# Bilinear row sampling as a sum of clamped ramps over row differences, in place of a sum of hats over rows

## The chip, the cores and the metric

The kernel runs on one core of a Trainium2 chip as one launch. The metric is the device time of that launch in microseconds. A core has five engines that work side by side, each through its own instructions in order: TensorE (PE in the profile, its weight loads PEld), VectorE (DVE), ScalarE (ACT), GpSimd (POOL) and SyncE (SP), which here only issues transfers.

## The reference

The reference is a network of four residual layers on x of shape (16, 32, 128, 128). Each layer adds a block of the group-normalised x. The change lies in layer 1, a deformable convolution with nine taps along a curved line. Cut to what matters:

```
x = x + L0(gn(x));  x = x + L1(gn(x));  x = x + L2(gn(x));  x = x + L3(gn(x))

def L1(input):                        # (16, 32, 128, 128)
    offset = tanh(group_norm(conv3x3(input)))
    y_off  = offset[:, :9]
    y      = weight * mamba(y_off) + rows + cumulated(y_off)   # 9 row maps
    x_new  = columns + (-4 .. 4)
    ys = clip(y, 0, 127);  xs = clip(x_new, 0, 127)
    deformed = grid_sample_bilinear(input, xs, ys)
    out = conv2d(deformed, dsc_w, dsc_b, stride=(9, 1))        # sum over 9 taps
    return group_norm(out, gn_w, gn_b, 8)
```

The columns xs are whole numbers, so the bilinear sample mixes two rows of one column. For tap k at column c it is the sum over all rows r of hat(ys - r) * input[r, c + k - 4], where hat(d) is 1 - |d| between -1 and 1 and 0 elsewhere.

## The kernel before, in words

The program runs its stages one after the other: `layer0` writes x1 to a scratch tensor in DRAM, `layer1_offsets` makes the offsets, `layer1_scan` runs the recurrence and writes the nine clipped row maps (ymap), `layer1_sample` (L1122) samples, convolves, normalises and writes x2, and layers 2 and 3 follow. x1 is kept in four tensors of 128 rows (four images of 32 channels each); one row holds a whole 128 x 128 image plane.

`layer1_sample` takes the 16 images one after the other, and each image in 32 blocks of four columns (HW // 4 = 32, numbered n; i is n modulo 4). The 128 partitions hold the image's rows r, so that a matmul contracts over rows: its weights are one column of the image (128 rows by 32 channels, from the tile xt), and its moving operand is the matrix of hats for 128 output points. Four such matmuls with different column groups fill one PSUM bank of 128 x 512.

The hats come in three ways, by tap:

- Taps 4 to 7: `fetch` (L1198) loads the row map of the block with the same 2048 numbers in all 128 partitions (tile yd, four buffers, 1 MB each). `absolutes` (L1331) lets ScalarE form |y - r| with a bias of minus the row number (nrow), and `hats` (L1215) lets VectorE form min(., 1) - 1, which is minus the hat. The convolution's weights w4 and w8 carry the factor -1.
- Taps 0 to 3: `near` (L1335) calls `spread` (L1206), where TensorE copies one row of the small tile Y to all partitions, two taps into each of two PSUM tiles pb (two buffers). ScalarE empties each with Abs into ya, and VectorE applies `hats`.
- Tap 8: `eighth` (L1340) does the same once in four blocks out of Y8, into h8.

`taps` (L1229) runs the 16 matmuls of four taps into a bank pd, and VectorE copies the bank into ds (L1371 after taps 0 to 3, L1377 after taps 4 to 7). `last_tap` (L1241) does tap 8 for four blocks, and ScalarE copies that bank (L1398). The banks pd have two buffers that go round. Once in four blocks `convolve` (L1252) multiplies with the convolution's weights, ScalarE adds the bias (oc, L1267), and one block later `turn` (L1270) transposes back to rows. `finish` (L1282) is a generator of which one step is taken per block; it normalises the previous image, adds xt (L1324) and stores x2 through POOL's queue. It runs from block 1 of the next image to block 22. xt has two buffers, and an image's buffer is given back only when `finish` has read it.

`open_image` (L1178), called at block 12 for the image after, issues the loads of Y, Y8 and xt on SP's queue. `in_order` (L1349) holds TensorE, VectorE and ScalarE to the order of the code; the order of SP's issues is left to the scheduler. The loop's body puts the work of block m in this order: taps 0 to 3 of m; Abs of yd and hats of ya for m + 1; the copy L1371; the spread of m + 2; taps 4 to 7 of m; hats of yd for m + 1; the copy L1377; then by i the convolution (0), the turn (1), the eighth tap's spread (2) or the last tap (3).

Of the kernel before, what the change touches and what calls it, by code (L numbers as in the profile page):

```python
# [68 lines left out]
def layer0(tc, w, x, x1, nb=B):  # L69
# [5 lines left out]
    with ExitStack() as ctx:  # L75
# [200 lines left out]
        def tail_z(st):  # L276
            b, t0 = st["b"], st["t0"]
            pz = ps_1.tile([P, 4, HW], F32, name="pz", tag="pz")
            for k in range(4):
                nc.tensor.matmul(pz[:, k], st["aT"][:, k], wadd, start=True, stop=False)  # L280
                nc.tensor.matmul(pz[:, k], st["mT"][:, k], wmod, start=False, stop=True)
            o = wp.tile([P, 4, HW], F32, name="o", tag="o")
            nc.vector.tensor_add(o, pz, xs[b][:, t0 : t0 + 4])
            r0 = (b % 4) * T + t0
            nc.sync.dma_start(x1[b // 4][r0 : r0 + 4].rearrange("t (c d) -> c t d", d=HW), o)

# [835 lines left out]
def layer1_sample(tc, w, x1, x2, ymap, sb1, batches=range(B)):  # L1122
# [8 lines left out]
    nc = tc.nc  # L1131
    V, S, M = nc.vector, nc.scalar, nc.tensor.matmul
    W4 = 4 * HW
    NB = HW // 4
    batches = list(batches)
    with ExitStack() as ctx:
# [8 lines left out]
        ident = load(nc, cp, w["ident"], "ident")  # L1145
        nrow = load(nc, cp, w["nrow"], "nrow")
        avg = cp.tile([P, P], F32, name="avg", tag="avg")
        V.memset(avg, 1.0 / P)

        sel = cp.tile([P, 32, P], F32, name="sel", tag="sel")  # L1150

        cb = cp.tile([P, NG, 4, 2], F32, name="cb", tag="cb")
        with tc.tile_pool(name="ct", bufs=1) as tp:
            e32 = load(nc, tp, w["eye32"], "eye32")
# [23 lines left out]
        def open_image(b):  # L1178
            im = images[b] = {}
            g, j = divmod(b, 4)  # L1180
            im["Y"] = Y = yp.tile([P, W4], F32, name="Y", tag="Y")
            nc.sync.dma_start(Y, ym(b)[0:4].rearrange("k (n f) -> (k n) f", f=W4))
            im["Y8"] = Y8 = yp.tile([P, W4], F32, name="Y8", tag="Y8")
            y8 = ym(b)[8].rearrange("(s q f) -> q s f", q=4, f=W4)
            for q in range(4):
                nc.sync.dma_start(Y8[32 * q : 32 * q + 8], y8[q])
            im["xt"] = xt = xp.tile([P, T, HW], F32, name="xt", tag="xt")
            xg = x1[g][T * j : T * j + T].rearrange("o (r c) -> r o c", c=HW)
            for q in range(4):
# [4 lines left out]
            V.tensor_scalar(w4, dw4[:, :, 0:T], s, -1.0, ALU.mult, ALU.mult)  # L1194
            im["w8"] = w8 = sp.tile([P, P], F32, name="w8", tag="w8")
            V.tensor_scalar(w8, dw8, s, -1.0, ALU.mult, ALU.mult)

# [7 lines left out]

        def spread(dst, Y, n, k):  # L1206

            for h in range(2):
                pb = psb.tile([P, 2, W4], F32, name="pb", tag="pb")
                for a in range(2):  # L1210
                    q = 32 * (2 * h + a)
                    M(pb[:, a], sel[q : q + k, n], Y[q : q + k], start=True, stop=True)  # L1212
                S.activation(dst[:, 2 * h : 2 * h + 2], pb, AF.Abs, bias=nrow)  # L1213

        def hats(t):  # L1215

            V.tensor_scalar(t, t, 1.0, 1.0, ALU.min, ALU.subtract)  # L1217

# [63 lines left out]
        def finish(b):  # L1282

            g, j = divmod(b, 4)
            im = images[b]
            ob, xt = im["ob"], im["xt"]
            st = sp.tile([P, 8, 6], F32, name="st", tag="st")
# [42 lines left out]

        def absolutes(m):  # L1331
            yd = blocks[m]["yd"]
            S.activation(yd, yd, AF.Abs, bias=nrow)  # L1333

        def near(m):  # L1335
            b, n = order[m]
            blocks[m]["ya"] = ya = hp.tile([P, 4, W4], F32, name="ya", tag="ya")
            spread(ya, images[b]["Y"], n, 32)

        def eighth(b, s):  # L1340
            h8 = hp.tile([P, 4, W4], F32, name="h8", tag="h8", bufs=2)
            spread(h8, images[b]["Y8"], s, 8)
            images[b]["h8", s] = h8

        open_image(batches[0])
        NM = len(order)
        for m in range(min(3, NM)):
            fetch(m)
        with in_order(tc, nc.tensor, nc.vector, nc.scalar):  # L1349
            eighth(batches[0], 0)  # L1350
            near(0)
            absolutes(0)
            near(1)
            hats(images[batches[0]]["h8", 0])
            hats(blocks[0]["ya"])
            hats(blocks[0]["yd"])
            done = iter(())
            for m in range(NM + 6):
                b, n = order[m] if m < NM else (None, m - NM)
                if m < NM:  # L1360
                    bl = blocks[m]
                    bl["ds"] = dp.tile([P, 2, W4], F32, name="ds", tag="ds", bufs=6)
                    if n == 12 and m + NB < NM:
                        open_image(order[m + NB][0])
                    if m + 3 < NM:
                        fetch(m + 3)
                    pd = taps(m, 0, bl["ya"])
                    if m + 1 < NM:
                        absolutes(m + 1)
                        hats(blocks[m + 1]["ya"])  # L1370
                    V.tensor_copy(bl["ds"][:, 0], pd.rearrange("p i r -> p (i r)"))  # L1371
# [5 lines left out]
                    V.tensor_copy(bl["ds"][:, 1], pd.rearrange("p i r -> p (i r)"))  # L1377
                s, i = divmod(n, 4)
# [16 lines left out]
                elif i == 3 and m < NM:  # L1395
# [3 lines left out]
                    images[b]["ds8"] = ds8  # L1399
                    if m + 1 < NM:  # L1400
                        nb_, nn = order[m + 1]
                        hats(images[nb_]["h8", nn // 4])
                next(done, None)
# [954 lines left out]
def network(ctx, tc, w, x, out):  # L2358
# [5 lines left out]

    x1 = [scratch([P, L], f"x1_{g}") for g in range(NG)]
    x2 = [scratch([P, L], f"x2_{g}") for g in range(NG)]
# [36 lines left out]
def pack(inp):  # L2403
# [203 lines left out]
```

## Time and profile before

| what | us |
|---|---|
| median of 3 runs | 16701.83 |
| lowest and highest of them | 16687.33, 16788.68 |
| the profiled execution's own time | 16668.54 |
| span in the profile | 16666.3 |
| first to last matmul of the spread (L1212) | 10735.9 to 13888.4 |
| last store issue of the sampling stage (L1325) | 13929.8 |
| SP's 14 waits for L1324 ahead of the xt loads | 64.4 |
| ScalarE's 14 waits for yd's load | 56.7 |

The span is the time from the first to the last instruction of the profiled execution. A row of the groups has the line, the engine, the operation, what it writes and reads with the shapes and the count, then the busy time in all and the mean of one in ns, then the idle time of the engine just before and what ended it. Matmuls are pipelined, so their mean is longer than their share of the time. A row of the waits has who waited, for whom, the total, how often, and the longest.

### The profile page before, as it was taken

The page shows a single profiled execution, that of the slowest core. Times are in us where ns is not written, and L with a number is a line of the kernel's source. Part 1 is how long each engine was busy: PE and PEld are TensorE (multiplying, and loading weights), DVE is VectorE, ACT ScalarE, POOL GpSimd, SP SyncE. Part 2 cuts the span into 40 slices and gives each one's busy share as a digit, 9 for nine tenths or more (in the row PEclk, how much of TensorE's full clock was granted, in tenths as well). Part 3 has the DMA queues.
Part 4 walks back from the last instruction along what each step waited for, and adds up shares of the span by engine and source line. Part 5 has one row for each costly group of instructions (what it writes and reads, how often), then busy time and mean ns, then how long its engine had stood idle before and what let it go on. Part 6 is the DMA issues. An engine that isn't in the chain of part 4 may idle for free. (4 is left out here: it accounts for less than half of the span.)

```text
span 16666.3 us, 327843 instructions
## 1 busy us (share of the span) xinstructions
PE 14464.2 (87%) x126810; PEld 5828.1 (35%) x126810; DVE 14412.7 (86%) x13784; ACT 12525.8 (75%) x25236; POOL 9711.4 (58%) x17789
## 2 busy tenths in 40 slices
PE   8998999989999888888888888899999997689966
PEld 3333333333333432222222222255555554434421
DVE  9999999999999659999999999888888886698622
ACT  8999999999999557777777777598888984466411
POOL 8999999999999457778887888500000001000012
PEclk9999999999999989999999999899899998789977
DMA  0000000000000334444454445578777876444356
GB/s 23 12 13 12 12 18 12 13 13 12 18 12 8 95 110 159 160 161 164 166 166 165 163 165 167 153 186 195 194 201 196 198 194 182 98 83 83 75 150 201
DMA packets 1347602, 1837.19 MB, mean 110 GB/s; under 512 B 161685, under 2 KB 661902, under 8 KB 1335799
## 3 DMA queue, kind: packets, MB, share of 16 engines
q1 hardware_dynamic: 1289910, 1655.23, 36.2%
q0 software_dynamic: 43840, 144.20, 2.4%
q8 instruction: 997, 16.33, 0.4%
q10 hardware_dynamic: 12288, 16.79, 0.4%
q14 instruction: 567, 4.64, 0.1%
HBM read 1497.44 MB, written 229.64 MB: 104 GB/s over the span
## 5 line engine op out<-in xcount | busy, mean ns | idle before, releaser
L235 POOL TENSOR_SCALAR Rp<-su,nv 128x128 f32<-128x128 f32 x15360 | 5406.6, 371 | 167.9 <-PE pS L241 133.0
L239 ACT ACTIVATE Ra<-su,bv 128x128 f32<-128x128 f32 x15360 | 4626.2, 390 | 406.7 <-PE pS L241 403.3
L224 DVE TENSOR_TENSOR Rd<-pu,nv 128x2048 f32<-128x2048 f32 x2176 | 4856.6, 2275 | 17.8 <-PE pS L241 16.8
L241 PE MATMUL pS<-Rd,zw 128*32 128x512 f32 x17408 | 2798.0, 606 | 378.7 <-DVE Rd L224 377.9
L919 DVE TENSOR_TENSOR_SCAN hh<-dd,state,pd 128x512 f32<-128x512 f32 x2304 | 2823.1, 1267 | 152.4 <-ACT ln L834 7.1
L940 POOL TENSOR_TENSOR hh<-hh,bc 128x2048 f32<-128x2048 f32 x512 | 2319.2, 4530 | 450.8 <-DVE state L927 439.8
L1325 POOL DMA_DIRECT2D x<-ob x64 | 92.0, 1438 | 3100.4 <-DVE ob L1324 2766.5
L904 PE MATMUL pd<-du,spread 32*128 32x512 f32 x4608 | 1340.1, 655 | 574.6 <-DVE hh L919 566.7
L896 ACT ACTIVATE dd<-dd,m_a 128x512 f32<-128x512 f32 x2304 | 1514.8, 713 | 335.3 <-DMA dd<-dm 328.9
L914 DVE TENSOR_TENSOR pd<-pd,bc 128x1024 f32<-128x1024 f32 x1152 | 1400.6, 1216 | 58.7 <-ACT bc L877 55.4
L241 PE MATMUL pS<-Rp,zw 128*32 128x512 f32 x7680 | 1314.3, 598 | 26.0 <-POOL Rp L235 25.9
L1333 ACT ACTIVATE yd<-yd,nrow 128x2048 f32<-128x2048 f32 x512 | 1238.1, 2418 | 56.7 <-DMA yd<-ymap 56.7
L1213 ACT ACTIVATE ya<-pb,nrow 128x1024 f32<-128x1024 f32 x1024 | 1196.7, 1260 | 80.6 <-PE pb L1212 80.1
L241 PE MATMUL pS<-Ra,zw 128*32 128x512 f32 x7680 | 1237.3, 601 | 0.0
L1212 PE MATMUL pb<-Y,sel 32*128 32x512 f32 (+1 forms) x5120 | 1075.3, 739 | 176.0 <-ACT ya L1213 172.8
L241 PEld LDWEIGHTS pS<-Rd,zw 128*32 128x32 f32 x17408 | 582.1, 109 | 1484.7 <-DVE Rd L224 927.4
L904 PEld LDWEIGHTS pd<-du,spread 32*128 32x128 f32 x4608 | 371.1, 189 | 1607.4 <-DVE hh L919 726.8
L1217 DVE TENSOR_SCALAR yd<-yd 128x2048 f32<-128x2048 f32 x512 | 727.5, 1421 | 207.0 <-ACT yd L1333 205.8
L1217 DVE TENSOR_SCALAR ya<-ya 128x2048 f32<-128x2048 f32 x512 | 759.0, 1482 | 10.7 <-ACT ya L1213 9.4
L1224 PE MATMUL pd<-ya,xt 128*32 128x128 f32 x16384 | 691.4, 311 | 42.5 <-DVE ds L1377 31.7
L1945 PE MATMUL ps<-t,W 128*128 128x512 f32 x1280 | 635.4, 644 | 80.9 <-DVE W L1925 53.1
L1224 PEld LDWEIGHTS pd<-yd,xt 128*32 128x32 f32 x16384 | 533.2, 178 | 471.0 <-issue 224.7
(434 smaller groups left out, 22927.2 us busy)
## 6 DMA issues: line engine op xcount, KB each, us to landing
dd<-dm SPq DMA_DIRECT2D x2304, 256.0 KB
yd<-ymap SPq DMA_DIRECT2D x512, 1024.0 KB
xq<-x SPq DMA_DIRECT2D x48, 1088.0 KB
dm<-dt POOLq DMA_DIRECT2D x192, 256.0 KB, 3.8
w<-d SPq DMA_DIRECT2D x512, 73.1 KB
xb<-tok SPq DMA_DIRECT2D x248, 144.0 KB
x<-in_x SPq DMA_DIRECT2D x64, 512.0 KB
x<-o SPq DMA_DIRECT2D x128, 256.0 KB
```

What stands on the lines that cost most here:

```text
L224: nc.vector.tensor_tensor(R, st["pu"].unsqueeze(1).to_broadcast([P, 4, 4, HW]), nv[:, :, i::32].rearrange("p t q -> p q t").unsqueeze(3).t ...
L235: nc.gpsimd.tensor_scalar(R[:, q, k], su[:, k], 3.4028234e38, nv[:, k, c], ALU.min, ALU.max)
L239: nc.scalar.activation(R[:, q, k], su[:, k], AF.Relu, bias=bv[:, k, c])
L241: nc.tensor.matmul(st["pS"][32 * q : 32 * q + 32], zw[:, 31 - i : 63 - i], R[:, q], start=first, stop=False, tile_position=(0, 32 * q), sk ...
L896: S.activation(dd[:, r], dd[:, r], AF.Exp, scale=acol[:, dr, d : d + 1])
L904: nc.tensor.matmul(pd[:, a], spread[e, k], st["du"][n][e], start=True, stop=True)
L914: V.tensor_mul(pd, pd, bm.unsqueeze(1).to_broadcast([P, 2, CH]))
L919: V.tensor_tensor_scan(hh[:, r, s], dd[:, r, s], pd[:, a, s], st["state"][:, 4 * i + r : 4 * i + r + 1], ALU.mult, ALU.add,)
L940: G.tensor_mul(hh, hh, st["bc"][1, n].unsqueeze(1).to_broadcast([P, 4, CH]))
L1217: V.tensor_scalar(t, t, 1.0, 1.0, ALU.min, ALU.subtract)
L1224: M(pd[32 * q : 32 * q + 32, i], xt[:, :, xc], h, start=True, stop=True, tile_position=(0, 32 * q),)
L1333: S.activation(yd, yd, AF.Abs, bias=nrow)
```

## The change

A sum over rows of hat(y - r) * x[r] is rewritten. With y between 0 and 127 it equals x[0] plus the sum over r of clamp(y - r, 0, 1) * (x[r + 1] - x[r]). Partitions 0 to 126 hold the differences, and partition 127 holds x[0] with a ramp that is always 1 (its entry in the bias is +1 in place of -127). To load rows 1 to 128 in one shifted transfer, `layer0` stores each plane's first row once more behind the last, so a row of x1 is 128 elements longer.

- xt is loaded shifted by a row. `differ` loads the unshifted rows a quarter at a time (tile xq) and subtracts them on GpSimd, at blocks 24 to 27 of the image before. `finish` no longer reads xt: it loads quarters of its own.
- The row number is subtracted by the spread product: one row of ones beside 16 rows of Y, and the row numbers beside the selector. Y is split into Y0 and Y1, and each group of 16 rows is loaded with its row of ones. VectorE clamps taps 0 to 3 straight out of PSUM (max 0, min 1), one instruction per pb.
- h8 is formed on ScalarE in two passes, relu(1 - v) and again relu(1 - .). Taps 4 to 7 take a Relu with the bias on ScalarE and a min with 1 on VectorE.
- The two copies of pd into ds go from VectorE to ScalarE. In the code the Relu of yd for m + 1 now stands behind the first copy and the spread of m + 2.
- GpSimd is held to the order of the code too.

```diff
@@ layer0
-            nc.sync.dma_start(x1[b // 4][r0 : r0 + 4].rearrange("t (c d) -> c t d", d=HW), o)
+            nc.sync.dma_start(x1[b // 4][r0 : r0 + 4].rearrange("t (c d) -> c t d", d=HW)[0:P], o)
+            nc.sync.dma_start(x1[b // 4][r0 : r0 + 4, L:].unsqueeze(0), o[0:1])
@@ layer1_sample, set-up
-        sel = cp.tile([P, 32, P], F32, name="sel", tag="sel")
+        sel = cp.tile([P, 16, P], F32, name="sel", tag="sel")
...
-            V.tensor_copy(sel, e32.unsqueeze(2).to_broadcast([P, 32, P]))
+            V.tensor_add(
+                sel, pick.unsqueeze(2).to_broadcast([P, 16, P]),
+                srow.unsqueeze(1).to_broadcast([P, 16, P]),
+            )
@@ open_image
-            im["Y"] = Y = yp.tile([P, W4], F32, name="Y", tag="Y")
-            nc.sync.dma_start(Y, ym(b)[0:4].rearrange("k (n f) -> (k n) f", f=W4))
-            im["Y8"] = Y8 = yp.tile([P, W4], F32, name="Y8", tag="Y8")
+            yk = ym(b)[0:4].rearrange("k (h n f) -> k h n f", h=2, f=W4)
             y8 = ym(b)[8].rearrange("(s q f) -> q s f", q=4, f=W4)
-            for q in range(4):
-                nc.sync.dma_start(Y8[32 * q : 32 * q + 8], y8[q])
+            for h, key in enumerate(("Y0", "Y1", "Y8")):
+                im[key] = Y = yp.tile([P, W4], F32, name=key, tag=key)
+                for q in range(4):
+                    p = 32 * q
+                    if h < 2:
+                        nc.sync.dma_start(Y[p : p + 16], yk[q, h])
+                    else:
+                        nc.sync.dma_start(Y[p : p + 8], y8[q])
+                        nc.sync.dma_start(Y[p + 8 : p + 16], y8[q])
+                nc.sync.dma_start(Y[16:P:32], w["one_rows"])
...
-                nc.sync.dma_start(xt[:, 8 * q : 8 * q + 8], xg[:, 8 * q : 8 * q + 8])
+                o = slice(8 * q, 8 * q + 8)
+                nc.sync.dma_start(xt[:, o], xg[1 : P + 1, o])
...
+        def quarter(b, q):
+            g, j = divmod(b, 4)
+            xq = xp.tile([P, 8, HW], F32, name="xq", tag="xq")
+            xg = x1[g][T * j + 8 * q : T * j + 8 * q + 8].rearrange("o (r c) -> r o c", c=HW)
+            nc.sync.dma_start(xq, xg[0:P])
+            return xq
+
+        def differ(b, q):
+            xt = images[b]["xt"][0 : P - 1, 8 * q : 8 * q + 8]
+            G.tensor_sub(xt, xt, quarter(b, q)[0 : P - 1])
@@ spread
-                    M(pb[:, a], sel[q : q + k, n], Y[q : q + k], start=True, stop=True)
-                S.activation(dst[:, 2 * h : 2 * h + 2], pb, AF.Abs, bias=nrow)
-        def hats(t):
-            V.tensor_scalar(t, t, 1.0, 1.0, ALU.min, ALU.subtract)
+                    M(pb[:, a], sel[q : q + 17, n], Y[q : q + 17], start=True, stop=True)
+                v = dst[:, 2 * h : 2 * h + 2]
+                if whole:
+                    V.tensor_scalar(v, pb, 0.0, 1.0, ALU.max, ALU.min)
+                else:
+                    S.activation(v, pb, AF.Relu, bias=one, scale=-1.0)
+                    S.activation(v, v, AF.Relu, bias=one, scale=-1.0)
+        def clamps(t):
+            V.tensor_scalar_min(t, t, 1.0)
@@ finish
+                xq = quarter(b, q)
...
-                V.tensor_add(ob[:, o], ob[:, o], xt[:, o])
+                V.tensor_add(ob[:, o], ob[:, o], xq)
@@ the loop
         open_image(batches[0])
+        for q in range(4):
+            differ(batches[0], q)
...
-        with in_order(tc, nc.tensor, nc.vector, nc.scalar):
+        with in_order(tc, nc.tensor, nc.vector, nc.scalar, nc.gpsimd):
...
+                    if 24 <= n < 28 and m + NB < NM:
+                        differ(order[m + NB][0], n - 24)
                     if m + 3 < NM:
                         fetch(m + 3)
                     pd = taps(m, 0, bl["ya"])
-                    if m + 1 < NM:
-                        absolutes(m + 1)
-                        hats(blocks[m + 1]["ya"])
-                    V.tensor_copy(bl["ds"][:, 0], pd.rearrange("p i r -> p (i r)"))
+                    S.copy(bl["ds"][:, 0], pd.rearrange("p i r -> p (i r)"))
                     if m + 2 < NM:
                         near(m + 2)
+                    if m + 1 < NM:
+                        ramps(m + 1)
                     pd = taps(m, 4, bl["yd"])
                     if m + 1 < NM:
-                        hats(blocks[m + 1]["yd"])
-                    V.tensor_copy(bl["ds"][:, 1], pd.rearrange("p i r -> p (i r)"))
+                        clamps(blocks[m + 1]["yd"])
+                    S.copy(bl["ds"][:, 1], pd.rearrange("p i r -> p (i r)"))
...
-                        hats(images[nb_]["h8", nn // 4])
@@ network, pack
-    x1 = [scratch([P, L], f"x1_{g}") for g in range(NG)]
+    x1 = [scratch([P, L + HW], f"x1_{g}") for g in range(NG)]
...
-    w["nrow"] = -np.arange(P, dtype=f)[:, None]
+    w["step"] = -np.arange(P, dtype=f)[:, None]
+    w["step"][P - 1] = 1.0
```

More of the change, by code (lines that the diff above doesn't have):

```diff
@@ L1131, in layer1_sample @@
     nc = tc.nc
-    V, S, M = nc.vector, nc.scalar, nc.tensor.matmul
+    V, G, S, M = nc.vector, nc.gpsimd, nc.scalar, nc.tensor.matmul
     W4 = 4 * HW
@@ L1145, in layer1_sample @@
         ident = load(nc, cp, w["ident"], "ident")
-        nrow = load(nc, cp, w["nrow"], "nrow")
+        step = load(nc, cp, w["step"], "step")
+        one = cp.tile([P, 1], F32, name="one", tag="one")
+        V.memset(one, 1.0)
         avg = cp.tile([P, P], F32, name="avg", tag="avg")
         V.memset(avg, 1.0 / P)
-        sel = cp.tile([P, 32, P], F32, name="sel", tag="sel")
+        sel = cp.tile([P, 16, P], F32, name="sel", tag="sel")
         cb = cp.tile([P, NG, 4, 2], F32, name="cb", tag="cb")
         with tc.tile_pool(name="ct", bufs=1) as tp:
-            e32 = load(nc, tp, w["eye32"], "eye32")
-            V.tensor_copy(sel, e32.unsqueeze(2).to_broadcast([P, 32, P]))
+            pick = load(nc, tp, w["pick"], "pick")
+            srow = load(nc, tp, w["step_row"], "step_row")
+            V.tensor_add(
+                sel, pick.unsqueeze(2).to_broadcast([P, 16, P]),
+                srow.unsqueeze(1).to_broadcast([P, 16, P]),
+            )
             selq = load(nc, tp, w["selq"], "selq")
@@ L1189, in open_image @@
             for q in range(4):
-                nc.sync.dma_start(xt[:, 8 * q : 8 * q + 8], xg[:, 8 * q : 8 * q + 8])
+                o = slice(8 * q, 8 * q + 8)
+                nc.sync.dma_start(xt[:, o], xg[1 : P + 1, o])
             s = cb[:, g, j, 0:1]
             im["w4"] = w4 = sp.tile([P, 2, T], F32, name="w4", tag="w4")
-            V.tensor_scalar(w4, dw4[:, :, 0:T], s, -1.0, ALU.mult, ALU.mult)
+            V.tensor_scalar_mul(w4, dw4[:, :, 0:T], s)
             im["w8"] = w8 = sp.tile([P, P], F32, name="w8", tag="w8")
-            V.tensor_scalar(w8, dw8, s, -1.0, ALU.mult, ALU.mult)
+            V.tensor_scalar_mul(w8, dw8, s)
+        def quarter(b, q):
[7 more added lines that the diff above has]
+            G.tensor_sub(xt, xt, quarter(b, q)[0 : P - 1])
         def fetch(m):
@@ L1204, in fetch, with spread @@
             )
-        def spread(dst, Y, n, k):
+        def spread(dst, Y, n, whole):
             for h in range(2):
@@ L1285, in finish @@
             im = images[b]
-            ob, xt = im["ob"], im["xt"]
+            ob = im["ob"]
             st = sp.tile([P, 8, 6], F32, name="st", tag="st")
@@ L1329, in finish, with ramps @@
                 yield
-        def absolutes(m):
+        def ramps(m):
             yd = blocks[m]["yd"]
-            S.activation(yd, yd, AF.Abs, bias=nrow)
+            S.activation(yd, yd, AF.Relu, bias=step)
         def near(m):
@@ L1337, in near @@
             blocks[m]["ya"] = ya = hp.tile([P, 4, W4], F32, name="ya", tag="ya")
-            spread(ya, images[b]["Y"], n, 32)
+            spread(ya, images[b][f"Y{n // 16}"], n % 16, True)
         def eighth(b, s):
             h8 = hp.tile([P, 4, W4], F32, name="h8", tag="h8", bufs=2)
-            spread(h8, images[b]["Y8"], s, 8)
+            spread(h8, images[b]["Y8"], s, False)
             images[b]["h8", s] = h8
         open_image(batches[0])
+        for q in range(4):
+            differ(batches[0], q)
         NM = len(order)
@@ L1348, in layer1_sample @@
             fetch(m)
-        with in_order(tc, nc.tensor, nc.vector, nc.scalar):
+        with in_order(tc, nc.tensor, nc.vector, nc.scalar, nc.gpsimd):
             eighth(batches[0], 0)
             near(0)
-            absolutes(0)
+            ramps(0)
             near(1)
-            hats(images[batches[0]]["h8", 0])
-            hats(blocks[0]["ya"])
-            hats(blocks[0]["yd"])
+            clamps(blocks[0]["yd"])
             done = iter(())
@@ L1399, in layer1_sample @@
                     images[b]["ds8"] = ds8
-                    if m + 1 < NM:
-                        nb_, nn = order[m + 1]
-                        hats(images[nb_]["h8", nn // 4])
                 next(done, None)
@@ L2508, in pack @@
     w["dsc_rows"] = np.tile(np.stack([i["gn_w"], i["gn_b"]])[None], (P, 1, 1))
-    w["nrow"] = -np.arange(P, dtype=f)[:, None]
+    w["step"] = -np.arange(P, dtype=f)[:, None]
+    w["step"][P - 1] = 1.0
+    w["pick"] = np.tile(np.eye(T, dtype=f)[:, :16], (4, 1))
+    w["step_row"] = np.zeros((P, P), f)
+    w["step_row"][16::T] = w["step"][:, 0]
+    w["one_rows"] = np.ones((4, 4 * HW), f)
     def conv(a):
```

## The prediction, made before the changed kernel ran

> **What bounds the kernel now.** Only the sampling stage changes much. The page says that no engine is free of work over the whole run:
>
> ```profile
> PE 14464.2 (87%) x126810; PEld 5828.1 (35%) x126810; DVE 14412.7 (86%) x13784; ACT 12525.8 (75%) x25236; POOL 9711.4 (58%) x17789
> ```
>
> The instructions of `layer1_sample` start at 10736 and its last stores leave at 13930. One window over the loop (columns: length, busy PE, PEld, DVE, ACT, POOL with counts, granted clock, DMA share, GB/s) shows three engines near 90%, so none is the bound by its sum:
>
> ```profile
> 10740.00:13905.00 3165.00, 2881.60 (x44864) 1694.47 (x44858) 2724.92 (x2893) 2802.59 (x2064) 88.49 (x60) 0.90 0.79 194
> ```
>
> The groups of that window give the price of each part:
>
> ```profile
> L1333 ACT ACTIVATE yd<-yd,nrow 128x2048 f32<-128x2048 f32 x512 | 1238.1, 2418 | 56.7 <-DMA yd<-ymap 56.7
> L1213 ACT ACTIVATE ya<-pb,nrow 128x1024 f32<-128x1024 f32 x1024 | 1196.7, 1260 | 80.6 <-PE pb L1212 80.1
> L1217 DVE TENSOR_SCALAR ya<-ya 128x2048 f32<-128x2048 f32 x512 | 759.0, 1482 | 10.7 <-ACT ya L1213 9.4
> ...
> L1371 DVE COPY ds<-pd 128x512 f32<-128x512 f32 x512 | 374.3, 731 | 89.0 <-PE pd L1224 88.0
> L1213 ACT ACTIVATE h<-pb,nrow 128x1024 f32<-128x1024 f32 x256 | 309.5, 1261 | 106.5 <-PE pb L1212 59.2 <-DMA nrow<-in_nrow 47.1
> ...
> L1398 ACT COPY ds<-pd 128x512 f32<-128x512 f32 x128 | 116.5, 910 | 32.9 <-PE pd L1224 32.4
> ```
>
> The waits show who holds whom: TensorE waits for ScalarE to empty the spread buffers (318.8 + 172.8), and for VectorE's copies (155.4 + 112.1):
>
> ```profile
> PEld pb L1212 <- ACT ya L1213: 318.8, 343, 6.2
> ...
> PE pb L1212 <- ACT ya L1213: 172.8, 129, 6.0
> PEld pd L1224 <- DVE ds L1377: 155.4, 233, 1.8
> PEld pd L1224 <- DVE ds L1371: 112.1, 148, 1.5
> ```
>
> ScalarE's timeline over one group of four blocks (oc to oc is 24.3 us) shows it nearly without gaps; its largest wait is for the convolution:
>
> ```profile
> 12057.02 0.90 ACT L1267 ACTIVATE oc<-po,bos 128x512 f32<-128x512 f32 x1 [0.99 <-PE po L1264]
> 12057.74 2.48 ACT L1333 ACTIVATE yd<-yd,nrow 128x2048 f32<-128x2048 f32 x1
> 12060.09 2.44 ACT L1213 ACTIVATE ya<-pb,nrow 128x1024 f32<-128x1024 f32 x2
> 12062.39 2.46 ACT L1333 ACTIVATE yd<-yd,nrow 128x2048 f32<-128x2048 f32 x1
> 12064.74 2.10 ACT L1213 ACTIVATE ya<-pb,nrow 128x1024 f32<-128x1024 f32 x2
> 12067.36 1.11 ACT L1213 ACTIVATE h<-pb,nrow 128x1024 f32<-128x1024 f32 x1 [0.52 <-PE pb L1212]
> ```
>
> The starts of yd, sorted by block, have median distances 5.70, 6.12, 4.70 and 7.15: 23.7 us for four blocks. That holds equally where VectorE carries the 1.4 us rows of `finish` and where it doesn't, so VectorE is not the bound; the hand-offs between ScalarE and TensorE are.
>
> **The main part: who empties which bank.** Per block the change takes from ScalarE two spread evacuations, and gives it two copies and, once in four blocks, two more passes over h8. I walk both orders through four blocks. Every engine takes its work in code order, and a hand-over costs 0.1. Durations are start-to-start distances from the timeline: taps 1.20, spread half 0.57, convolution 2.98, turn 0.66, last taps 1.10; ScalarE yd 2.35 (12062.39 to 12064.74), spread half 1.12, a 512-wide bank 0.70 (L1267 above). A 1024-wide pass from SBUF is not in the trace; half of L1333 gives 1.2. TensorE's sum is 20.04 in both orders.
>
> Before, from the end of the convolution at 6.52, ScalarE goes through oc (7.32), yd (9.67), a spread (11.91), yd (14.26), a spread (16.50), h8 (18.74) and yd (21.09); VectorE's clamp of that yd (1.25) and its copy (0.60) free the bank at 23.04, and the next group's taps start at 23.14 (measured 23.7). After (T TensorE, S ScalarE, c copy):
>
> ```
> i=0 T taps 0-1.20, spread -2.34, taps -3.54, conv -6.52
>     S c 1.30-2.00, yd -4.35, c -5.05
> i=1 T taps 6.52-7.72, spread -8.86, taps -10.06, turn -10.72
>     S oc 6.62-7.32, c 7.82-8.52, yd -10.87, c -11.57
> i=2 T taps 10.72-11.92, spread -13.06, taps -14.26, h8 -14.83, 15.20-15.77
>     S c 12.02-12.72, yd -15.07, c -15.77, h8 15.77-16.89,
>       16.99-18.19, 18.19-19.31, 19.41-20.61
> i=3 T taps 15.77-16.97, spread 16.99-17.56, 19.41-19.98, taps -21.18,
>       last taps 21.41-22.51
>     S c 20.61-21.31, yd -23.66, c -24.36
> i=0 T taps 24.46
> ```
>
> The next taps need the bank that the copy at 24.36 frees. So four passes over h8 stand between a copy and the bank it empties, and TensorE, which VectorE's quick copies let run ahead, now stands twice for about 1.9 us. Four blocks take 24.46, **+1.32; times 128, +169 us**. Bounds: a copy at L1398's shortest (0.55), yd at its shortest (2.0) and the h8 passes at 1.06 give 22.76, −49 us; copies at L1398's mean 0.91 give 25.30, +277. I take 0.70, the start-to-start value. VectorE loses 0.96 us a block (two copies, 1.48 for ya, 0.43 for h8, against two clamps out of PSUM at 1.21, by L914's 1216 ns at the same width): cover, not path. Queued behind each waiting copy on ScalarE is the yd ramp, and behind that VectorE's clamp; its reader is the next block's second taps, in the walk 6 to 8 us later, so it delays nothing.
>
> **Clock.** Windows after a wait show what TensorE's gaps cost:
>
> ```profile
> 12208.25:12209.00 0.75, 0.00 (x0) 0.00 (x0) 0.75 (x3) 0.75 (x2) 0.00 (x0) 1.00 0.77 268
> ...
> 12210.50:12211.25 0.75, 0.75 (x20) 0.75 (x16) 0.72 (x3) 0.70 (x1) 0.00 (x0) 0.50 1.04 191
> ```
>
> After about 1.9 us without work the clock stood near 0.5 for 3.7 us. The 0.56 between walk and measurement holds such spells. TensorE's idle per four blocks grows from 3.1 to 4.4; scaled alike, 0.56 becomes 0.80: **+30 us** (0 to half a spell more, 0.95 × 128 = +122). The Trainium skill (TensorE: Matmul & The Clock Gate, What's actually happening) has the clock drop only after an idle window of about 3.4 us; by that the gaps would be free and this term 0, but the row shows a gap of 1.9 us to be enough.
>
> A rule that speaks against the change: the Trainium skill (ScalarE: Activation LUTs, Rules for kernel authors) gives relu, min and add to VectorE, up to about 3x faster in bf16. Here copies differ by 0.70 against 0.60; at three times 0.60 the eight copies would add 8.8 us to four blocks, over 1100 us.
>
> **Loads.** An image issues 31 DMAs on SP instead of 9 (19 for Y, 4 xt, 8 quarters): 22 × 0.3 = 7 us, behind 4.0 us that SP waits per block for a free yd buffer (1954.5 / 488); uncovered, 105. The eight quarters add 4.2 MB to 38.5 MB per image; at 194 GB/s for a share of 0.79 the image needs 174 us of DMA in 200. Against this: today xt waits 64.4 us in all for L1324, the yd issues behind it come late, and ScalarE loses 56.7 us. With `finish` reading its own quarters, xt is free from the last tap on. **−45 us** (−57, to +60 if the eight loads hold yd up as the four of xt do).
>
> **The rest.** POOL's four subtractions per image (L938, same width: 2.35) stand in blocks 24 to 27, after the last store of `finish`, behind POOL's idle 97%; their reader is the next image's first taps, 24 us on. The first image has no such cover: 9.4 us, two quarters that wait for a buffer, and 3 at the tail, **+18** (10 to 35). VectorE's add in `finish` waits for a quarter issued two blocks (12 us) before; a store of the same size lands in 10.1 us at the median: 0. Layer 0's 128 extra stores, 0.36 each, stand behind SP's 4178.9 us of waits for L283: 0 (46 bare). Spreading with 17 rows instead of 32: 0, since the 8-row and 32-row forms have the same mean (737 and 739).
>
> **Sum:** 169 + 30 − 45 + 18 = +172. Against the profiled execution's 16668.5 that is 16840; the median of the runs shown, 16701.8, lies 33 higher, so **16874 us**, +1.0%.
>
> **Rivals.**
> 1. ScalarE is quicker after a copy than back to back (yd took 2.0 after a gap, 2.49 in the median), walk 22.76: −49 + 0 − 45 + 18 = −76, 16626, no slower than before. Against: yd still overlaps the taps. It decides if yd's mean falls under 2.1 and the copies' under 0.6. Chance 0.24.
> 2. VectorE was the true bound, and its copies' 267 us of TensorE waits go without return: 16702 − 267 − 45 + 18 = 16408. Against: `finish` blocks cost nothing extra. It decides if the banks come free before TensorE asks. 0.10.
> 3. Yd comes late at the quarters too: 16874 + 45 + 60 = 16979. Speaks for it: share 0.79 already. 0.16.
> The forecast itself: 0.50.
>
> **Numbers.** About 1% (167 us) can be told from no change. Slower: rival 3 (0.16) and 0.32 of the forecast's 0.50, which centres just above that line. Faster: rival 2 (0.10) and a tail of rival 1 (0.03). Same: the rest, 0.18 + 0.21. So faster 0.13, same 0.39, slower 0.48. The forecast's own range is 16800 (copies at 0.55: a walk of 23.86, 77 less) to 16980 (copies at 0.91: 25.30, 108 more). The range for all cases reaches from rival 1 to rival 3 with the copies half-way to 0.91 (+54): 16620 to 17040. It leaves out rival 2 and the ends of the two outer cases.
>
> **What would show it.** Right: four blocks at 24.5 to 25.3; taps waiting for ACT ds for over 300 us; DVE under 75% of the stage; a pb wait on ACT h in each group of four; clock under 0.90. Wrong: yd or copies shorter than 2.1 and 0.6, or ScalarE waiting for yd<-ymap over 120 us.

## The result and the profile after

The changed kernel takes 16948.9 us in the median of four runs, against 16743.2 us for the kernel before on the same chip: a ratio of 1.0124, 95% interval 1.0084 to 1.0165, or +206 us. The forecast was +172. In the later sessions the median of before lay between 16715 and 16747 us, so kernels of different sessions are compared by their ratio to before.

The busy line of the page, to be held against the first line shown of before:

```profile
PE 14712.7 (87%) x126810; PEld 6019.8 (36%) x126810; DVE 14113.3 (83%) x13145; ACT 12300.9 (73%) x25492; POOL 9857.6 (58%) x17853
```

VectorE and ScalarE have less to do than before, and the instruction count of TensorE is the same, yet its busy time rose by 248 us. One window over the sampling loop (columns as in the prediction) shows where:

```profile
10740.00:14220.00 3480.00, 3131.85 (x44944) 1882.67 (x44940) 2465.69 (x2315) 2582.71 (x2326) 257.71 (x136) 0.83 0.77 197
```

VectorE fell from 86% of this window to 71%, ScalarE from 89% to 74%, and the granted clock from 0.90 to 0.83. The stage is longer with two engines freed.

The groups of the same window answer to those of before. Each row has the busy time, the mean of one in ns, and the idle time just before:

```profile
L1240 DVE TENSOR_SCALAR ya<-pb 128x1024 f32<-128x1024 f32 x1024 | 1323.9, 1336 | 773.5 <-PE pb L1237 770.8 <-DMA xt<-x 1.9
L1364 ACT ACTIVATE yd<-yd,step 128x2048 f32<-128x2048 f32 x512 | 1269.5, 2479 | 75.8 <-DMA yd<-ymap 74.7 <-DVE ob L1307 1.0
...
L1243 ACT ACTIVATE h<-h,one 128x1024 f32<-128x1024 f32 x256 | 316.3, 1235 | 8.4
L1409 ACT COPY ds<-pd 128x512 f32<-128x512 f32 x512 | 315.1, 615 | 57.9 <-PE pd L1254 56.7
L1401 ACT COPY ds<-pd 128x512 f32<-128x512 f32 x512 | 310.3, 606 | 214.8 <-PE pd L1254 211.7
```

VectorE now empties the spread buffers (L1240), and it waits 770.8 us for TensorE to fill them. So no engine has too much to do in all: TensorE, VectorE and ScalarE wait for each other in turn. Who TensorE waits for is seen in the waits (total, times, longest):

```profile
PEld pd L1254 <- ACT ds L1401: 293.9, 370, 1.7
PEld pb L1237 <- DVE ya L1240: 246.2, 235, 2.7
...
PE pb L1237 <- DVE ya L1240: 124.8, 111, 1.7
PEld pb L1237 <- ACT h L1242: 114.5, 112, 5.7
...
ACT yd L1364 <- DMA yd<-ymap: 74.7, 17, 10.5
```

The first row is the weight load's wait; it lies mostly under running matmuls, since the matmuls of L1254 themselves stood idle for copies and clamps only 19 us in all (11.2 and 8.1). The third row is the matmul's own idle time, 111 times, about once in each of the 128 groups of four blocks. The timeline of one group shows where it comes from (start, length, engine, line; in brackets the idle time before and its releaser):

```profile
12210.41 1.20 DVE L1247 TENSOR_SCALAR yd<-yd 128x2048 f32<-128x2048 f32 x1
...
12211.54 0.67 DVE L1307 COPY ob<-pt 128x512 f32<-128x512 f32 x1
...
12212.14 1.25 DVE L1351 TENSOR_TENSOR ob<-ob,sc 128x1024 f32<-128x1024 f32 x1
...
12213.31 2.33 DVE L1240 TENSOR_SCALAR ya<-pb 128x1024 f32<-128x1024 f32 x2
...
12214.57 2.26 PE L1237 MATMUL pb<-Y,sel 17*128 17x512 f32 x8 [1.59 <-DVE ya L1240]
...
12215.74 1.11 ACT L1242 ACTIVATE h<-pb,one 128x1024 f32<-128x1024 f32 x1 [2.09 <-PE pb L1237]
...
12216.76 1.91 PE L1254 MATMUL pd<-ya,xt 128*32 128x128 f32 x32
...
12218.59 2.91 PE L1237 MATMUL pb<-Y,sel 17*128 17x512 f32 x8
...
12220.46 0.56 ACT L1401 COPY ds<-pd 128x512 f32<-128x512 f32 x1
```

VectorE has a clamp, the copy of ob and a step of `finish` to do before it comes to the two buffers of the third block; so the spread of h8, which needs the same two buffers, stands for 1.59 us. Then ScalarE goes through its four passes over h8 (12215.74 to 12220.56), and the copy of the fourth block's first taps ends at 12221.02. And 2.5 us after the standstill has ended TensorE falls to half its clock:

```profile
12213.00:12214.50 1.50, 0.00 (x0) 0.00 (x0) 1.50 (x3) 0.65 (x2) 0.00 (x0) 1.00 1.04 382
...
12217.00:12223.50 6.50, 6.50 (x80) 4.24 (x80) 4.07 (x4) 6.17 (x6) 0.00 (x0) 0.51 0.65 218
```

Three possible causes therefore lie in one place: VectorE's lateness, ScalarE's passes, and the clock. The experiments were to tell them apart.

**How long is which block.** ScalarE's ramp over yd runs once a block. The distances between its starts, taken from ScalarE's timeline, say which block is long. Medians in us by block (the distance that ends in the first, second, third, fourth block of a group); the mean length of four blocks; both without the first and the last eight blocks; and the clock granted between 10900 and 13800:

| kernel | ratio to before | clock | first, second, third, fourth | mean of four |
|---|---|---|---|---|
| before | 1 | 0.91 | 5.74, 6.09, 4.70, 7.24 | 24.45 |
| after | 1.0124 [1.0084, 1.0165] | 0.84 | 5.46, 6.13, 3.96, 9.73 | 26.29 |
| after, h8 by VectorE | 1.0118 [1.0089, 1.0148] | 0.83 | 6.86, 6.13, 3.96, 8.44 | 25.92 |
| before, h8's second pass on ScalarE | 1.0109 [1.0081, 1.0137] | 0.90 | 5.09, 6.21, 4.68, 9.59 | 26.01 |
| after, matmuls ahead of h8 | 1.0168 [1.0140, 1.0195] | 0.91 | 4.52, 6.13, 3.97, 10.55 | 26.69 |
| after, three steps a group | 1.0082 [1.0053, 1.0111] | 0.89 | 5.14, 6.14, 3.97, 8.85 | 25.46 |
| after, h8 behind the convolution | 1.0157 [1.0129, 1.0184] | 0.87 | 5.62, 11.33, 4.38, 3.77 | 26.51 |
| the same, by VectorE | 1.0055 [1.0038, 1.0073] | 0.91 | 6.28, 7.63, 5.55, 3.78 | 24.91 |
| after, second pass later | 1.0127 [1.0102, 1.0152] | 0.85 | 4.46, 6.19, 3.97, 10.33 | 25.81 |
| second pass later, three steps | 1.0051 [1.0032, 1.0069] | 0.90 | 4.44, 6.20, 3.96, 8.90 | 25.11 |
| second pass later, matmuls ahead | 1.0177 [1.0151, 1.0203] | 0.95 | 4.34, 6.20, 3.97, 10.33 | 26.38 |

From before to after only the fourth grows, by 2.49; the first and the third give 0.28 and 0.74 back. The mean of four rose by 1.84, times 128 groups 235 us.

The profile of after is 280 us longer than that of before; the profiled execution of before, 16668.5 us, lies 75 under the median of its runs, so the medians differ by less. Of the 280, from the first oc to the last it is 232 and from the scan to the first taps 27; the rest is 10 shorter. The other 32 arose in the scan ahead of the loop, whose code the change leaves alone; its last matmuls start anywhere from 10731 to 10859 us in the fourteen profiles of this study. So this part says nothing of the change, and what an edit does to the loop is better read from the mean of four than from the whole time.

### The profile page after: what moved, and what is told of

Same layout as the page of the kernel before. It is cut to its first block, busy times and chain, and to the rows that moved or that the text cites. A ratio compares the mean times of both kernels' runs of the same rounds, so it can differ in the third digit from the quotient of the medians.

```text
span 16946.8 us, 328647 instructions
## 1 busy us (share of the span) xinstructions
PE 14712.7 (87%) x126810; PEld 6019.8 (36%) x126810; DVE 14113.3 (83%) x13145; ACT 12300.9 (73%) x25492; POOL 9857.6 (58%) x17853
## 4 chain that ended last, share of the span: by engine, by line
DVE 34%; PE 31%; issue 15%; ACT 11%; POOL 4%; SPq 3%; DMA 3%; DVEq 0%; ACTq 0%; POOLq 0%
DVE hh L920 12%; DVE Rd L224 8%; PE pS L241 7%; ACT Ra L239 6%; DVE pd L915 5%; PE ps L1974 4%; PE ps L512 3%; PE pd L1254 3%; POOL Rp L235 3%; PE pb L1237 3%; PE pd L905 1%; DVE ya L1240 1%; SPq L2322 1%; PE ps L2179 1%; ACT dd L897 1%
## 5 line engine op out<-in xcount | busy, mean ns | idle before, releaser
L1240 DVE TENSOR_SCALAR ya<-pb 128x1024 f32<-128x1024 f32 x1024 | 1323.9, 1336 | 773.5 <-PE pb L1237 770.8
L1364 ACT ACTIVATE yd<-yd,step 128x2048 f32<-128x2048 f32 x512 | 1269.5, 2479 | 75.8 <-DMA yd<-ymap 74.7
L1237 PE MATMUL pb<-Y,sel 17*128 17x512 f32 x5120 | 1142.9, 759 | 173.8 <-DVE ya L1240 124.8
L1254 PE MATMUL pd<-ya,xt 128*32 128x128 f32 x16384 | 725.0, 323 | 48.6 <-POOL xt L1221 19.8
L1254 PEld LDWEIGHTS pd<-yd,xt 128*32 128x32 f32 x16384 | 584.0, 180 | 505.3 <-ACT ds L1401 291.4
L1254 PE MATMUL pd<-yd,xt 128*32 128x128 f32 x16384 | 727.7, 323 | 21.5 <-DVE yd L1247 8.1
```

The lines of the kernel that those rows point to most:

```text
L1237: M(pb[:, a], sel[q : q + 17, n], Y[q : q + 17], start=True, stop=True)
L1240: V.tensor_scalar(v, pb, 0.0, 1.0, ALU.max, ALU.min)
L1254: M(pd[32 * q : 32 * q + 32, i], xt[:, :, xc], h, start=True, stop=True, tile_position=(0, 32 * q),)
```

## The experiments

**h8 emptied by VectorE, in its place.** The kernel after, with one word changed:

```diff
-            spread(h8, images[b]["Y8"], s, False)
+            spread(h8, images[b]["Y8"], s, True)
```

> The changed kernel with h8 clamped by VectorE straight out of PSUM, as the taps 0 to 3 are; nothing else differs. Theory A (ScalarE's four passes over h8 stand between a copy and the bank that it empties, TensorE then idles and its clock drops): ScalarE is relieved of 4.8 us in each group of four blocks, the group falls from 25.8 us to 23.0 to 23.8, the granted clock in the stage rises from 0.83 to 0.89 or more, and the time falls by 2.0 to 2.8 us x 128 = 260 to 360, to 16600 to 16700. Theory B (VectorE empties the spread buffers too late, which the trace shows as 371 us of TensorE waits ahead of the h8 spread): two more rows of 1.3 us per group on VectorE make it later, and the time stays within 60 of 16949.

Measured: 16928.6 us, by its ratio the same as after: theory B's time, not theory A's. ScalarE's four passes are gone, and the fourth block is 1.3 us shorter, but VectorE's two more passes make the first of the next group 1.4 longer; the mean of four is 0.37 shorter, 47 us over 128 groups. The passes alone were not what could be had back.

**The copies of pd back on VectorE.** The kernel after, with both copies into ds as before:

```diff
-                    S.copy(bl["ds"][:, 0], pd.rearrange("p i r -> p (i r)"))
+                    V.tensor_copy(bl["ds"][:, 0], pd.rearrange("p i r -> p (i r)"))
...
-                    S.copy(bl["ds"][:, 1], pd.rearrange("p i r -> p (i r)"))
+                    V.tensor_copy(bl["ds"][:, 1], pd.rearrange("p i r -> p (i r)"))
```

> The changed kernel with both copies of pd into ds back on VectorE. If the move of the copies to ScalarE were the cost by itself, the time falls back to 16700 to 16800. By theory A it does not: VectorE's second copy stands behind the clamp of yd, which waits for the ramp, which stands behind ScalarE's four passes over h8; a walk of the four blocks gives 26 to 27.4 us against 24 to 25.8, so 17000 to 17250, and taps wait for DVE ds in place of ACT ds.

Measured: 17387.1 us, ratio 1.0377 [1.0340, 1.0414], outside of what was expected on the slow side. With VectorE emptying the spread and the copies in this order, they are far better on ScalarE; moving them by itself was no part of the loss.

**One piece of the change alone: h8's second pass on ScalarE.** The kernel before, in which VectorE's `hats` over h8 is replaced by two more passes of ScalarE:

```diff
+            for h in range(2):
+                v = h8[:, 2 * h : 2 * h + 2]
+                S.activation(v, v, AF.Relu, bias=one, scale=-1.0)
...
-                        hats(images[nb_]["h8", nn // 4])
```

> The kernel before with one part of the change alone: the second step of h8 runs on ScalarE, as relu(1 - .) over the two halves, in place of VectorE's min and subtract; w8 loses its factor -1. Theory A: ScalarE, nearly without gaps before, gets 2.3 us more per group and hands every bank of the next block on later; the walk gives 26.0 to 27.3 us for the group against 23.1 to 23.6, so 2.5 to 3.7 x 128 = 320 to 470 us more: 17060 to 17210. If ScalarE's passes were not on the path, VectorE's relief of 1.7 us per group would show: 16600 to 16750.

Measured: 16921.0 us against 16727.5, +194 us. The expectation of theory A was higher; but this one piece, put into the order of before, costs nearly what the whole change costs. Its fourth block is 9.59, as after (9.73), and its clock over the stage is that of before (0.90 and 0.91):

```profile
10900.00:13800.00 2900.00, 2558.79 (x39087) 1484.23 (x39090) 2194.05 (x2411) 2668.87 (x2020) 76.10 (x52) 0.90 0.76 183
```

In the fourth block itself the clock is lower than in that of before, 0.80 against 0.88 in the mean. But the 12 fourth blocks that ran above 0.9 have a median of 9.78 us, and the 59 below 0.8 one of 9.81. So a fourth block of this length arises at either clock.

**The image's buffer free early.** The kernel before, in which `finish` loads quarters of its own, so that xt is given back sooner:

```diff
+                xq = quarter(b, q)
...
-                V.tensor_add(ob[:, o], ob[:, o], xt[:, o])
+                V.tensor_add(ob[:, o], ob[:, o], xq)
```

> The kernel before with another part alone: finish loads its own quarters of x1, so that the buffer of xt is free from the last tap on; no differences, no other change. Prediction's step: SP no longer waits for L1324 ahead of the xt loads, ScalarE's waits for yd's load fall from 57 us to under 15, time 16680 to 16720. Rival (SP is held up by the quarters that wait for a free xq buffer, and the yd issues behind them come late): ScalarE's waits for yd's load stay at 50 to 100 us, time 16740 to 16800.

Measured: 16720.5 us, ratio 0.999 [0.9974, 1.0007]. ScalarE's wait for yd falls from 56.7 to 39.6 us, between the two ranges named; so even the wait itself gives back only 17.

**TensorE kept busy through the standstill.** The kernel after, with eight matmuls of no use ahead of h8's spread:

```diff
+                    fl = pso.tile([P, 4, P], F32, name="fl", tag="pt")
+                    for r in range(8):
+                        M(fl[:, r % 4], ident, ident, start=True, stop=True)
                     eighth(nb_, nn // 4)
```

> Theory C (the clock): once in every group of four blocks TensorE stands still for about 1.6 us ahead of the spread of h8, since VectorE empties the two banks of that block late, and two to four us later the granted clock is 0.50 for 7 to 10 us; that half-clock stretch is where the loop's +227 us are. Here eight matmuls of 128x128 on the identity, with no use, are put on TensorE just ahead of the spread of h8, so that it works (by the transposes' 0.165 us each about 1.1 to 1.3 us) where it stood still; nothing of VectorE's or ScalarE's order changes. Theory C expects the sampling stage's granted clock to rise from 0.84 to 0.88 or more, and 16700 to 16850 us although work was added. Theory V (TensorE is paced by VectorE's emptying, and the clock is only along for the ride): clock 0.82 to 0.85, 16930 to 17100 us.

Measured: 16992.1 us. The clock did what theory C expected, 0.84 to 0.91; the time did not. The window of after and of this kernel:

```profile
10900.00:13800.00 2900.00, 2671.38 (x38660) 1612.08 (x38660) 2096.65 (x1948) 2226.42 (x2002) 197.00 (x104) 0.84 0.78 202
```

```profile
10900.00:13800.00 2900.00, 2680.44 (x39780) 1713.28 (x39778) 2077.57 (x1919) 2191.69 (x1970) 201.07 (x104) 0.91 0.78 198
```

The waits for the spread buffers in these windows, after first:

```profile
PE pb L1237 <- DVE ya L1240: 107.7, 96, 1.7
PEld pb L1237 <- ACT h L1242: 97.0, 97, 5.7
...
PE pb L1237 <- ACT h L1242: 39.0, 35, 5.2
```

```profile
PEld pb L1237 <- ACT h L1242: 244.3, 178, 5.8
...
PE pb L1237 <- ACT h L1242: 132.6, 142, 5.5
```

The matmuls' own wait for VectorE is gone (107.7 us in after, 1.0 here), and a wait for ScalarE's passes has come in its place: a faster TensorE only reaches the buffers that ScalarE still holds. The eight matmuls took 2.05 us at full clock, not the 1.1 to 1.3 expected, so by this estimate they fill the 1.59 us and add 0.46, 59 us over 128 groups. The mean of four grew by 0.40, 51 us, about as much; so no gain of note from the higher clock shows.

**VectorE early by one step.** The kernel after, in which `finish` takes no step behind the second block of a group:

```diff
-                next(done, None)
+                if i != 1:
+                    next(done, None)
```

> The finishing step (one pass over a quarter, 1.2 to 1.6 us on VectorE, or a pair of statistics) that stands behind the second block of a group is left to the later blocks, so that VectorE has three steps per group in place of four and reaches the emptying ahead of h8's spread 1.2 to 1.6 us earlier. Theory C (the wait ahead of h8 halves the clock): that wait of about 1.6 us shrinks to under 0.5, the stage's clock rises from 0.84 to 0.88 or more, 16700 to 16850 us. Theory V (VectorE paces the loop as a whole): its work is the same, the wait moves to another block; 16900 to 17000 us, clock 0.82 to 0.85.

Measured: 16859.0 us, just above theory C's range. Its profile's loop is 104 us shorter than that of after and the fourth block 0.88 shorter; the intervals of the two ratios overlap a little, so the profile's row carries the verdict. The matmuls' own wait for VectorE, between 10900 and 13800 as above:

```profile
PE pb L1237 <- DVE ya L1240: 51.7, 113, 0.6
```

The wait is 0.46 us in the mean and 0.6 at most, where under 0.5 was expected, and the clock rose to 0.89. As a higher clock alone gave nothing with the eight matmuls, the gain is put down to VectorE's lateness: some 0.8 to 0.9 us a group. This run alone doesn't tell the two apart.

**h8 behind the convolution, by ScalarE and by VectorE.** The kernel after, with the spread of h8 moved to where TensorE has the convolution between two spreads:

```diff
-            eighth(batches[0], 0)
...
-                elif i == 1 and 5 <= m <= NM + 1:
+                if i == 0 and m < NM:
+                    eighth(b, s)
+                if i == 1 and 5 <= m <= NM + 1:
...
-                elif i == 2 and m + 2 < NM:
-                    nb_, nn = order[m + 2]
-                    eighth(nb_, nn // 4)
```

> The spread of h8 is moved from behind the third block of the group before to behind the convolution of its own group, where TensorE has about 3 us of other matmuls between the spread of ya and that of h8; ScalarE empties it in two passes as in the kernel after. Theory C: no wait for VectorE ahead of h8, clock 0.88 or more, 16650 to 16850 us. Theory A (ScalarE's four passes, 4.8 us in a row, are what costs): they now hold up the copies of the next block, 16900 to 17050 us.

> As the kernel with h8's spread behind the convolution, and VectorE empties h8 in one pass each (2.6 us a group in place of ScalarE's 4.8). Theory C: 16550 to 16800 us, clock 0.89 or more, the best of the four if VectorE has room (its share of the stage was 0.72). Theory V: VectorE is later still in the block behind, the wait for ya grows there, 16900 to 17050 us.

Measured: 16971.6 us with ScalarE's passes, 16810.3 with VectorE's. The first shows that the long block goes where h8 goes: now the second is 11.33 and the fourth 3.77. Theory C fell there (the clock rose to 0.87 without gain) and theory A gave the time. The second, which takes the passes from ScalarE and gives VectorE a place where it is less late, gave 139 us back by the medians and 0.7% (some 115 us) by the ratios, though not to the range that theory C named; its mean of four is 1.38 shorter than that of after. With h8 in its old place the same emptying gave 0.37, and the new place with ScalarE's passes gave nothing. It is the place and the engine together. The clock rose along with it, to 0.91, and what part that has in the gain was not tested.

**h8's second pass later.** The kernel after; the two first passes stand together, and one second pass over 128x2048 follows the next copy:

```diff
-                    S.activation(v, v, AF.Relu, bias=one, scale=-1.0)
...
+                    if n % 4 == 3:
+                        h8 = images[b]["h8", n // 4]
+                        S.activation(h8, h8, AF.Relu, bias=one, scale=-1.0)
```

> ScalarE still does h8 in two passes, but its two first passes, which empty the banks, now stand together, and the second pass, one over 128x2048, follows one copy later, ahead of block four's ramp. The second bank of h8 is free some 1.2 us earlier and the copy that follows some 2.3 us earlier; no work is taken away. Theory D (a chain in order paces the fourth block: VectorE empties ya late, then h8's spread, then ScalarE's passes, then the spread of the next ya, then VectorE; when TensorE is kept busy in it, as with the eight matmuls put in, the time stays): 1.2 us x 128 groups off the loop of 3330 us, 16740 to 16880 us. Theory V (VectorE alone sets the chain's length): 16900 to 17000 us.

Measured: 16930.7 us, in theory V's range. The mean of four fell by 0.48, 61 us over 128 groups, where theory D asked for 1.2 in each: it fell for this edit alone. The waits for ScalarE's passes shrink (97.0 to 46.7 for the weight loads between 10900 and 13800), those for VectorE stay.

**The same with three steps a group.**

> Both ends of the chain at once: h8's second pass later, and no finishing step of VectorE behind the second block of a group (which alone took about 90 us off). Theory D: the two add up, 16650 to 16790 us, and ramps waiting for yd's load grow over 200 us in all, as they did with the step moved alone (214 us). If one of the two had only uncovered the other: no better than the better of them, 16790 to 16880 us.

Measured: 16806.1 us, 143 below after by the medians and 0.7% by the ratios. That is just over theory D's range and inside the other, which was to show that one edit had only uncovered the other; yet the mean of four fell by 1.18, and by 0.48 and 0.83 for each edit alone, so in the loop the two nearly add up. ScalarE's waits for yd reach 221.9 us in 78 times: with shorter groups the loads come late.

**The quarters on GpSimd's queue.** The kernel with both edits, and one more:

```diff
-            nc.sync.dma_start(xq, xg[0:P])
+            nc.gpsimd.dma_start(xq, xg[0:P])
```

> As the kernel with both edits, and the loads of the quarters (xq) are issued on GpSimd's queue in place of SP's, so that no load of yd stands behind a quarter that waits for its buffer. Rival 3 of the prediction (yd late behind the quarters): the ramps' waits for yd fall below 60 us and 50 to 130 us come off against the kernel with both edits alone. If the loads are late for another reason, or ScalarE has room to take them late: the same within 40 us; slower than that if GpSimd, which now waits for the buffers itself, subtracts or stores late.

Measured: 16948.3 us, 142 more than without this edit, as the last case named has it. ScalarE's wait for yd is all but gone, 2.1 us in place of 221.9, but the quarters themselves are late (waits between 10740 and 14220):

```profile
DVE ob L1354 <- DMA xq<-x: 256.6, 14, 24.0
...
PE pd L1253 <- POOL xt L1221: 74.6, 11, 26.6
```

VectorE's last step of `finish` and the next image's first taps now wait for what GpSimd issues and subtracts late. The quarters do hold yd up on SP's queue, as rival 3 had it; on GpSimd's queue they cost the loop more: it is 54 us longer from the first taps to the last. That is not all of the 142. In the two profiles, 160 us apart, 91 arose in the scan ahead of the loop, and whether the edit has a part in that isn't shown.

**Matmuls ahead and second pass later, together.**

> Two edits that gave nothing alone, together: the eight matmuls with no use ahead of h8's spread (alone: stage clock 0.91, but 16992 us, TensorE then waiting for ScalarE's passes) and h8's second pass put behind the next copy (alone: no wait for ScalarE left, but stage clock 0.85 and 16931 us). Theory E (two limits side by side in the fourth block, the half clock and ScalarE's four passes, of which the longer counts): only together do they give time back, 16740 to 16860 us, though the eight matmuls add 1.1 to 2 us of work to each of 128 groups. Theory V (VectorE, late by its finishing step and the copy of ob, sets the length of the group whatever the other two do): 16900 to 17000 us.

Measured: 17025.1 us at a stage clock of 0.95, the highest of all; above both ranges. Theory E fell. The matmuls' waits for the spread buffers are down to 40.0 us for ScalarE; between 10900 and 13800 TensorE now waits 108.6 us for the copies and 61.0 for h8's second pass ahead of the last taps:

```profile
PE pd L1253 <- ACT ds L1411: 108.6, 89, 1.3
...
PE pd L1253 <- ACT h L1403: 61.0, 99, 1.6
```

The fourth block is 10.33, the same as without the eight matmuls at a clock of 0.85.

No kernel built on after was as fast as before; the two nearest, h8's second pass later with three steps a group and h8 behind the convolution by VectorE, are 0.5% slower. The second has the shortest loop, 24.91 us for four blocks against 24.45 before. Where the rest of their time lies was not taken apart further.

## Why the prediction was right, point by point

**Main part, +169: the right mechanism, sized too low, since VectorE's own queue was left out of the walk.** By the walk's starts of yd (2.00, 8.52, 12.72, 21.31, 26.46) its four distances, the one into the fourth block last, are 5.15, 6.52, 4.20 and 8.59; measured were 5.46, 6.13, 3.96 and 9.73. Three agree to 0.4, and the fourth, where the four passes over h8 stand, is 1.14 short. The prediction let h8's spread follow the third block's taps at once, at 14.26, with 0.37 us of wait between its halves; in the timeline it stood 1.59 us before its first half, because VectorE first has the clamp, the copy of ob and a step of `finish`. "VectorE loses 0.96 us a block (...): cover, not path" is the sentence that failed: VectorE has less to do, but what it does now stands between two spreads, in order, and each of its passes out of PSUM took 1.34 us in the mean, not 1.21. Taking one step from ahead of it gave 0.88 of the 1.14 back. That ScalarE's passes lengthen the fourth block is shown by the kernel before with the second pass alone (7.24 to 9.59).

**Clock, +30: the fall was larger (0.91 to 0.84), and no run shows that it cost time by itself.** Filling the gap raised the clock to 0.91, and with the second pass later to 0.95, without a gain; and with the second pass put into the kernel before, the fourth block was as long at a high clock as at a low one. In the fourth block TensorE has slack while it waits for others; at half clock it seems to spend that slack as busy time. A small part stays open. In after itself the 23 fourth blocks above a clock of 0.9 have a median of 9.24 us and the 74 below 0.8 one of 9.83: if the clock alone made this difference, and not what else sets these blocks apart, it would be some 45 us over the loop, an estimate. The Trainium skill (Perfetto Trace Analysis, Matmul Optimizations) says that the matmul engine scales its power with its use, so that matmuls should run back to back in batches. The traces agree as to the clock (0.84 to 0.91 with the gap filled, 0.85 to 0.95 where h8's second pass also stood later) and show no gain in time from it. TensorE's 92% of busy time between 10900 and 13800 thus left more room than it seemed to.

**Loads, −45: wrong in sign.** ScalarE's wait for yd rose from 56.7 to 74.7 us, and giving xt back early, done alone, changed the time by −0.1% with an interval that holds zero. The quarters hold yd up after all; but these waits are small against the loop, and with them all but gone the kernel with the quarters on GpSimd's queue was no faster. No run shows the 45 us as a gain.

**The rest, +18.** From the scan's last matmuls to the first taps it was 39.2 us and is 65.7, +27 in place of some 15; the first taps of before and after:

```profile
10770.09 2.02 PE L1224 MATMUL pd<-ya,xt 128*32 128x128 f32 x32 [1.28 <-DMA xt<-x]
```

```profile
10828.06 2.00 PE L1254 MATMUL pd<-ya,xt 128*32 128x128 f32 x32 [19.79 <-POOL xt L1221]
```

GpSimd's subtraction of the first image has no cover, as was said, and it came later than said; its 64 subtractions took 2.79 us in the mean, not 2.35. The stretch is 64 to 67 us in after and the kernels with its set-up, 73 where GpSimd issues the quarters, and 38 to 39 in before and the two built on it.

**Sum.** 169 + 30 − 45 + 18 = 172 met +206, but not term by term. The loop grew by 235 where 169 + 30 − 45 = 154 were forecast, and its start by 27 where 15 were. These add up to more than 206; the profiled execution of before, from which the terms were read, was a short one. The total was right with better luck than its parts.

**The rivals.** ScalarE quicker after a copy: the copies came near its mark (0.606 and 0.615 us, with 0.70 assumed and under 0.6 asked for), yd did not (2479 ns in the mean against 2418), and the condition asked for both. VectorE the true bound: it lost 15 points of its share and the kernel became slower. Yd late at the quarters: seen, at 18 us more of waits, not the 105 priced.

**The marks.** VectorE under 75% (71%), a wait for h in each group (112 of 128) and a clock under 0.90 came as named. So did the taps' wait for ScalarE's copies: 293.9 us for the first copy and 16.7 for the second are over the 300; as they are weight loads' waits, mostly under running matmuls, it was a poor mark. Four blocks, 24.5 to 25.3: the four medians add up to 25.28, measured as the 23.7 of the prediction was, just inside; the mean of four, 26.29, with its longer groups, is not.

## What to carry to other kernels

When work is moved from a full engine to one with room, walk all engines in order, those that get lighter too: what counts is what stands ahead of the moved instruction in its new queue. A low clock or a high busy share of TensorE in a stretch where it waits for others may be only the form that its slack takes; fill the gap, and see whether the time moves, before calling it the cause. Where limits lie side by side in one block, taking away one gives nothing or only a part (at most 0.83 of the 1.84 us by which four blocks had grown); two of them taken away at once gave 1.18, and moving the work itself, here h8's emptying to a place and an engine with room, gave 1.38.

## What the runs showed of the hardware

- A standstill of TensorE of 1.6 us was followed, 2.5 us after it had resumed, by some 7 us at a clock of 0.50 (the two windows above). The Trainium skill (TensorE: Matmul & The Clock Gate, What's actually happening) has the clock fall after an idle window of about 3.4 us; in this case's windows it fell behind a standstill of less than half of that.
- Such a standstill was not enough by itself, though the prediction took one of 1.9 us to be enough. Of the standstills of 1.3 to 2.2 us at full clock between 10900 and 13800, 50 of 58 in after were followed by half clock within 3.5 us, but only 9 of 76 in the kernel before with h8's second pass on ScalarE. What else it takes isn't shown.
- Eight 128x128 matmuls of float32 on the identity took 2.05 us at full clock, 0.26 us each and listed as 16 instructions; four transposes of the same size took 0.66, 0.165 each.
- ScalarE copied 512 columns out of PSUM in 606 ns in the mean, VectorE before in 731.
